# Both ends of a compressed-interaction kernel: the first weight row is loaded and summed earlier, and the last piece becomes 8 samples

## The chip, the cores and the metric

The kernel runs on one core of a Trainium2 chip. Its metric is the device time of one execution, in microseconds (us); four runs of the kernel before gave 485.12 to 485.51, median 485.37. One execution was profiled. The engines are named as the profile names them: PE (TensorE, the matrix products) and PEld (its weight loads), DVE (VectorE), ACT (ScalarE), POOL (GpSimd) and SP (SyncE, which here only issues transfers).

## The reference

A compressed interaction network of three layers over x, of shape (1024 samples, 64 fields, 16 embedding columns), all in float32:

```
x0 = h = x
for i in 0, 1, 2:                      # 128 output channels each
    z = einsum('bfe,bge->bfge', x0, h) # all pairs of fields
    y = einsum('oc,bce->boe', W_i, z.reshape(B, f0 * fh, E)) + b_i
    if i < 2: x_i, h = y[:, :64], y[:, 64:]
    else:     x_i = h = y
pooled = sum over e of concat(x_0, x_1, x_2)
out = pooled @ fc_w.T + fc_b           # (1024, 1)
```

The result is one number per sample. Since everything after layer 1 enters it only through fc_w, the kernel folds layer 2 and the pooled halves of the layers into small weight matrices, which it makes at its start.

## The kernel before

**Tiling.** The 1024 samples are 32 chunks of CB = 32 samples. A chunk has N = 512 columns (32 samples by 16 embedding columns). The pairs of fields of a chunk are 16 tiles of 128 rows by 512 columns: NJ = 4 groups j of NI = 4 tiles. The tiles of a group are one product on DVE or POOL (function product, L232): xa, the chunk's fields in four rotations, times one rotated copy xb of it, broadcast over the four. On PE, contract (L250 to L257) multiplies each of the 16 tiles of z by a 128x128 tile of w_all and adds them up in PSUM. The profile has two records, each with a weight load of its own (PEld), for one such float32 product.

**The start.** W0 comes in group by group as wh (the first tile row, 256 KB) and w0r (the other three, 768 KB). For each group, h1_weights (L352) adds the two mirrored halves of W0, one of which ACT first copies to PSUM (w0o). The first four chunks in HEAD order (2, 3, 0, 1) run a first half of the work (half_contract, L295) while the folded weights are made: PE makes the shifted copies xp of chunk 2 and 3 out of xa (L202), the products of W2 and W1 run between them (L408, L432), the result goes through DRAM (md) and comes back as ms, and DVE adds it into w_all (L531). After that head_q (L313) finishes chunks 0 and 1, and the other chunks go through contract.

**Order.** The order is written out by hand: each engine runs its instructions as the program lists them, and the loads are issued by SP in the order of load_xa, load_xb and the other dma_start calls. A transfer uses one of eight semaphores in turn, so a transfer can also wait for the landing of the one that used its semaphore last. The first transfers are xa of chunk c0 (first quarter, then the other three quarters), wh, the first quarter of xa of chunk c1, w0r, and so on.

**Around the change at the start** (L358 to L380): ACT copies a shifted tile for POOL (xb_gps), POOL multiplies group 1 of chunk c0 in two halves, DVE makes the products of group 0 for tile 0, then tile 1, then w_all's first row (after ACT's copy to w0o[0]), then the products for tiles 2 and 3. half_contract(c0, 0) on PE needs both.

**The end.** The last chunk, 31, is accumulated in two pieces (parts, in new_acc), 16 samples or 256 columns each (H2). For each chunk or piece, factors (L323) has ACT copy q out of PSUM (L329) and DVE multiply (L335); sums (L342) reduces over the 16 embedding columns (L344) into acc. pool (L605) sums over the channels by a product with ones on PE, into po; finish (L612) adds the constant cst on ACT and issues the output transfer. Before the change, the quarters of the output for all pairs of chunks but the last are pooled between the groups j = 1 and j = 2 of the second piece, and finished beside the rest of it. The last pair of chunks follows after the second piece: ACT copy, DVE product, DVE sum, pool on PE, bias on ACT, transfer on ACT's queue.

Of the kernel before, what the change touches and what calls it, by code (L numbers as in the profile page):

```python
# [37 lines left out]
F32 = mybir.dt.float32  # L38
AF = mybir.ActivationFunctionType
ALU = mybir.AluOpType  # L40
# [5 lines left out]
CB = 32  # L46
N = CB * E
H2 = N // 2
NCH = B // CB
NI = 4  # L50
NJ = 4
# [12 lines left out]
def cin_kernel(ctx, tc, xra, xrb, wh, w0r, w1h, w2t, wx1, wx0, vec, out):  # L64
# [109 lines left out]
    w2s = [flat_tile(f"w2_{k}") for k in range(2)]  # L174
    w1s = set_tile("w1s")
    load_xa(c0, slice(0, 1))
    load_xa(c0, slice(1, 4))
    nc.sync.dma_start(out=w0t[:, 0, :], in_=wh)
    load_xa(c1, slice(0, 1))
    nc.sync.dma_start(out=w0t[:, 1:NJ, :], in_=w0r)  # L180
    load_xa(c1, slice(1, 4))
# [35 lines left out]
    def new_acc(c, n=N, tag="acc"):  # L217
        if c == NCH - 1:
            parts[c] = [
                (ps.tile([128, H2], F32, tag=tag, name=f"acc_{c}_{n}", bufs=bufs), cols)  # L220
                for n, (tag, bufs, cols) in enumerate(
                    (("acc", 4, slice(0, H2)), ("set", 2, slice(H2, N)))
                )
            ]
            return
        accs[c] = ps.tile([128, n], F32, tag=tag, name=f"acc_{c}", bufs=4 if tag == "acc" else 2)

    def product(c, j, first=0, last=NI, engine=nc.vector):
        if first == 0:
            zs[c, j] = z_tile(f"z_{c}_{j}")  # L230
        at = slice(first, last)
        engine.tensor_tensor(  # L232
            zs[c, j][:, at, :], xas[c][:, at, :],
            xbs[c][j].unsqueeze(1).to_broadcast([128, last - first, N]), ALU.mult,
        )
        if j == NJ - 1:
            nc.scalar.activation(zs[c, j][SQ, 0, :], xas[c][SQ, 0, :], AF.Square)  # L237
# [12 lines left out]
    def contract(c, j, piece=0):  # L250
        acc_c, cols = pieces(c)[piece]
        for i in tiles(j):
            t = j * NI + i
            nc.tensor.matmul(  # L254
                acc_c, w_all[:, t, w_cols(c)], zs[c, j][:, i, cols],
                start=(t == 0 and c % 4 < 2), stop=(t == NT - NI and c % 4 >= 2),
            )  # L257
# [65 lines left out]
    def factors(c, which=slice(0, 1)):  # L323

        uu = uu_tile(c // 2)[halves[c % 2], 0, :]
        h = halves[c % 2]
        for acc_c, cols in pieces(c)[which]:
            q = sp.tile([128, N], F32, tag="q", name=f"q_{c}_{cols.start}")
            nc.scalar.copy(q[h, cols], acc_c[64 - h.start : 128 - h.start])  # L329
# [5 lines left out]
            nc.vector.scalar_tensor_tensor(  # L335
                uu[:, cols], acc_c[h], bh1[h], q[h, cols], ALU.add, ALU.mult
            )
# [4 lines left out]
    def sums(k, rows=slice(0, 128), of=slice(0, 2), half=slice(0, CB)):  # L342

        nc.vector.tensor_reduce(  # L344
            acc[rows, of, k, half],
            uus[k][rows, of, E * half.start : E * half.stop].rearrange("p k (b e) -> p k b e", e=E),
            AX.X,
            ALU.add,
        )

    def h1_weights(j, other=None):
        nc.vector.tensor_tensor(  # L352
            w_all[:, j * NI : (j + 1) * NI, 0:64], w0s[j][:, :, 0, :],
            w0s[j][:, :, 1, :] if other is None else other, ALU.add,
        )


    new_acc(c0, H2)  # L358
    nc.scalar.copy(xb_gps[:, 0, :], xbs[c0][1])  # L359
    xbs[c0][1] = xb_gps[:, 0, :]  # L360
    for i in (0, 2):
        product(c0, 1, i, i + 2, engine=nc.gpsimd)
    w0p = ps.tile([128, 2, NI, F], F32, tag="set", name="w0p")
    w0q = misc.rearrange("p (j i g) -> p j i g", i=NI, g=F)
    w0o = [w0p[:, 0], w0p[:, 1], w0q[:, 0], w0q[:, 1]]
    product(c0, 0, 0, 1)
    product(c0, 0, 1, 2)
    nc.scalar.copy(w0o[0], w0s[0][:, :, 1, :])
    h1_weights(0, w0o[0])
    product(c0, 0, 2, NI)  # L370
    nc.scalar.copy(w0o[1], w0s[1][:, :, 1, :])
    product(c0, 2, 0, 2)
# [232 lines left out]
    def pool(k0, k1, part=0, **flags):  # L605
        g, at = k0 // QP, slice(k0 % QP, (k1 - 1) % QP + 1)
        nc.tensor.matmul(  # L607
            po[32 * g : 32 * g + 2, at, :], ones, acc[:, part, k0:k1, :],
            tile_position=(0, 32 * g), skip_group_check=True, **flags,
        )  # L610

    def finish(k0, k1, queue):  # L612
        g, at = k0 // QP, slice(k0 % QP, (k1 - 1) % QP + 1)
        rows = slice(32 * g, 32 * g + 2)
        nc.scalar.activation(
            res[rows, at, :], po[rows, at, :], AF.Identity, bias=cst[rows]
        )
        queue.dma_start(out=outs[:, k0:k1, :], in_=res[rows, at, :])


# [1 line left out]
    for s, c in enumerate(order):  # L622
        k, head = c // 2, c in HEAD
        if order[s - 1] in HEAD and not head:
            for n in range(NF // 2):
                x_v0x(n)
            for n in HEAD:
                factors(n)
                if n % 2:
                    sums(n // 2)  # L630
        if 0 < s < len(order) - 2 and s not in (2, 3):
            load_products(*order[s + 2 : s + (4 if s == 6 else 3)])
        if s in (2, 3):

            if s == 2:
                for n in order[4:6]:
                    load_chunk(n)
                load_shared(0)
            for j in (0, 1) if s == 2 else (2, 3):
                for n in order[4:6]:  # L640
                    product(n, j)
        if s == len(HEAD) + 5:

            pc = ps.tile([128, 1], F32, tag="set", name="pc")
            for j in range(2):
                nc.tensor.matmul(
                    pc, fcol[:, j : j + 1].to_broadcast([128, 128]), bcol[:, j : j + 1],
                    start=(j == 0), stop=(j == 1),
                )
# [31 lines left out]
    po = ps.tile([128, QP, CB], F32, tag="set", name="po")  # L681
    quarters = [(k, min(k + QP, NP - 1)) for k in range(0, NP, QP)]
# [91 lines left out]
```

## Time and profile before

| what | value |
|---|---|
| median of four runs | 485.37 us |
| the profiled execution's own time | 485.12 us |
| its span in the profile | 483.3 us |
| PE busy | 477.2 us, 99% of the span |
| DVE, ACT, POOL busy | 368.8, 67.3, 15.3 us |
| bytes moved, mean rate | 87.01 MB, 180 GB/s |
| first product of half_contract on PE | 7.36 us |
| end of the last product column | 479.19 us |
| start of the last output transfer's issue | 481.27 us |

The profile is one execution. Its span begins with the first instruction and ends with the last; 1.8 us of the execution's time lie around it. A busy PE is not a PE at its peak, since products are pipelined. "The chain" is the work that ended last, followed back step by step to what released it: time that is on it counts, and time of an engine off it costs nothing unless something else then waits.

### The profile page before, as it was taken

Reading aid. Unit: us, or ns where it says so; the run is one execution under the profiler, and the core shown is the slowest. Engines: PE = TensorE matmul, PEld = TensorE weight load, DVE = VectorE, ACT = ScalarE, POOL = GpSimd, SP = SyncE. Lnnn points to the kernel's source line nnn. Section 1 sums busy time; section 2 is a strip of 40 time slices with the busy share of each in tenths; the row PEclk is TensorE's granted clock in tenths of the full one; section 3 lists DMA queues with packets and bytes.
Section 4 is the critical chain, followed back from the end, with each engine's and each line's share of the span. In section 5 each row is a group of like instructions: output and inputs, shape, how many; then the busy total and the mean of one; then the engine's idle time right before and its main releaser. Section 6 shows DMA issues by size and latency. Waiting matters only on the chain.

```text
span 483.3 us, 4409 instructions
## 1 busy us (share of the span) xinstructions
PE 477.2 (99%) x1802; PEld 217.3 (45%) x1802; DVE 368.8 (76%) x227; ACT 67.3 (14%) x142; POOL 15.3 (3%) x15
## 2 busy tenths in 40 slices
PE   8999999999999999999999999999999999999996
PEld 4564344443344444444444444444444444444465
DVE  5993799998899988898887686766868677771312
ACT  3242033011110111001100101001010011000002
POOL 5330000000000000000000000000000000000000
PEclk9999999999999999999999999999999999999999
DMA  8985997662952682587246344463246540000000
GB/s 335 403 277 175 391 378 279 219 215 108 353 236 87 228 285 111 196 268 283 107 171 210 142 174 175 171 213 105 120 174 224 210 147 28 0 1 0 0 1 1
DMA packets 19514, 87.01 MB, mean 180 GB/s; under 512 B 4802, under 2 KB 5474, under 8 KB 10598
## 3 DMA queue, kind: packets, MB, share of 16 engines
q1 hardware_dynamic: 18434, 85.71, 48.8%
q10 hardware_dynamic: 1060, 1.02, 0.8%
q8 instruction: 14, 0.23, 0.2%
q14 instruction: 6, 0.05, 0.0%
HBM read 85.08 MB, written 1.64 MB: 179 GB/s over the span
## 4 chain that ended last, share of the span: by engine, by line
PE 97%; DMA 1%; DVE 1%; ACT 0%; SPq 0%; issue 0%
PE acc L254 80%; PE acc L313 6%; PE acc L295 6%; PE acc L270 3%; PE acc L283 1%; DMA w0t<-in_wh 1%; PE xp L202 0%; PE pm L432 0%; PE pv L408 0%; PE y L275 0%; DVE z L232 0%; SPq L135 0%; PE po L607 0%; DVE uu L335 0%; DVE acc L344 0%
## 5 line engine op out<-in xcount | busy, mean ns | idle before, releaser
L254 PE MATMUL acc<-z,w_all 128*128 128x512 f32 (+1 forms) x928 | 387.5, 579 | 0.0
L232 DVE TENSOR_TENSOR z<-xa,xb 128x2048 f32<-128x2048 f32 x124 | 278.3, 2287 | 41.8 <-PE acc L254 35.1
L254 PEld LDWEIGHTS acc<-z,w_all 128*128 128x128 f32 x928 | 175.4, 190 | 210.8 <-issue 204.4
L237 ACT ACTIVATE z<-xa 32x512 f32<-32x512 f32 x34 | 21.3, 626 | 336.8 <-DVE z L232 334.8
L335 DVE SCALAR_TENSOR_TENSOR uu<-acc,vs,q 64x512 f32<-64x512 f32 (+1 forms) x29 | 21.2, 731 | 58.0 <-ACT q L329 57.8
L295 PE MATMUL acc<-z,w_all 128*64 128x256 f32 x256 | 29.0, 381 | 1.3 <-DVE w_all L352 1.3
L313 PE MATMUL acc<-z,w_all 128*64 128x512 f32 x128 | 27.9, 593 | 0.0
L232 DVE TENSOR_TENSOR z<-xa,xp 128x2048 f32<-128x2048 f32 (+2 forms) x12 | 20.4, 1749 | 5.3 <-PE xp L202 5.3
L295 PEld LDWEIGHTS acc<-z,w_all 128*64 128x64 f32 x256 | 17.9, 137 | 13.5 <-issue 2.5
L329 ACT COPY q<-acc 64x512 f32<-64x512 f32 (+1 forms) x33 | 18.7, 567 | 37.4 <-PE acc L254 21.4
L344 DVE TENSOR_REDUCE acc<-uu 128x64 f32<-128x1024 f32 (+3 forms) x19 | 20.3, 1073 | 0.3
L313 PEld LDWEIGHTS acc<-z,w_all 128*64 128x64 f32 x128 | 9.1, 137 | 18.0 <-issue 16.8
L275 PE MATMUL y<-xr,v0w 32*64 32x512 f32 x128 | 15.9, 600 | 0.0
L270 PE MATMUL acc<-xr,v1w 32*64 32x512 f32 (+1 forms) x132 | 15.7, 587 | 0.0
L340 DVE SCALAR_TENSOR_TENSOR uu<-y,cx,xx 128x512 f32<-128x512 f32 x16 | 11.3, 747 | 0.2
L270 PEld LDWEIGHTS acc<-xr,v1w 32*64 32x64 f32 x132 | 5.1, 131 | 9.9 <-issue 9.6
L232 POOL TENSOR_TENSOR z<-xa,xb_gps 128x1024 f32<-128x1024 f32 (+1 forms) x3 | 9.3, 3105 | 4.4 <-ACT xb_gps L359 3.8
L283 PE MATMUL acc<-sq,w_sq 32*64 32x512 f32 (+1 forms) x132 | 8.7, 574 | 0.0
L531 DVE TENSOR_TENSOR w_all<-ms 128x256 f32<-128x256 f32 x4 | 1.6, 424 | 5.2 <-DMA ms<-md 5.1
L166 ACT ACTIVATE sq<-xr 128x512 f32<-128x512 f32 x8 | 5.0, 630 | 3.5 <-DMA xr<-in_xra 3.3
L283 PEld LDWEIGHTS acc<-sq,w_sq 32*64 32x64 f32 x132 | 3.4, 132 | 3.8 <-issue 3.5
L232 POOL TENSOR_TENSOR z<-xa,xb 128x2048 f32<-128x2048 f32 x1 | 4.6, 4581 | 13.9 <-DMA xb<-in_xrb 13.9
(56 smaller groups left out, 66.8 us busy)
## 6 DMA issues: line engine op xcount, KB each, us to landing
xa<-in_xra SPq DMA_DIRECT2D x32, 1024.0 KB, 4.9
xb<-in_xrb SPq DMA_DIRECT2D x31, 1024.0 KB, 7.6
xr<-in_xra SPq DMA_DIRECT2D x32, 128.0 KB, 7.5
xx<-in_xra SPq DMA_DIRECT2D x32, 128.0 KB, 7.7
w<-in_w2t SPq DMA_DIRECT2D x2, 1024.0 KB, 10.9
xa<-in_xra SPq DMA_DIRECT2D x2, 768.0 KB, 7.9
w1s<-in_w1h SPq DMA_DIRECT2D x1, 1024.0 KB
w1x<-in_wx SPq DMA_DIRECT2D x1, 1024.0 KB
```

Of the source, the lines that this page charges most:

```text
L232: engine.tensor_tensor(zs[c, j][:, at, :], xas[c][:, at, :], xbs[c][j].unsqueeze(1).to_broadcast([128, last - first, N]), ALU.mult,)
L237: nc.scalar.activation(zs[c, j][SQ, 0, :], xas[c][SQ, 0, :], AF.Square)
L254: nc.tensor.matmul(acc_c, w_all[:, t, w_cols(c)], zs[c, j][:, i, cols], start=(t == 0 and c % 4 < 2), stop=(t == NT - NI and c % 4 >= 2),)
L270: nc.tensor.matmul(acc_c[halves[1 - n]], v1w[at, m], xr[:, cols], start=(m == 0 and c not in ends), stop=False, tile_position=(at.start, 6 ...
L275: nc.tensor.matmul(ys[c // 2][halves[n]], v0w[at, m], xr, start=(m == 0), stop=(m == 1), tile_position=(at.start, 64 * n),)
L283: nc.tensor.matmul(acc_c[halves[n]], w_sq[at, w_cols(c)][:, 64 * n : 64 * n + 64], sqs[first][at, cols], start=h and (first == 0 or c not ...
L295: nc.tensor.matmul(accs[c][halves[n]], w_all[:, t, 0:64], zs[c, j][:, i, n * H2 : (n + 1) * H2], start=(t == 0), stop=(j == last and i == ...
L313: nc.tensor.matmul(accs[c][halves[1 - c % 2]], w_all[:, t, 64:128], zs[c, j][:, i, :], start=(t == 0), stop=False,)
L329: nc.scalar.copy(q[h, cols], acc_c[64 - h.start : 128 - h.start])
L335: nc.vector.scalar_tensor_tensor(uu[:, cols], acc_c[h], bh1[h], q[h, cols], ALU.add, ALU.mult)
L340: nc.vector.scalar_tensor_tensor(uu_tile(k)[:, 1, :], ys[k], cx, xxs[k], ALU.add, ALU.mult)
L344: nc.vector.tensor_reduce(acc[rows, of, k, half], uus[k][rows, of, E * half.start : E * half.stop].rearrange("p k (b e) -> p k b e", e=E), ...
```

## The change

At the start, wh is loaded as the second transfer, directly after the first quarter of chunk c0's xa, and the rest of that xa follows as two transfers (one quarter, then two). ACT's copy to w0o[0] and DVE's sum of w_all's first row stand before xb_gps and before the first product. POOL's group is three products (two tiles, one, one) instead of two.

At the end, the two pieces of chunk 31 have 24 and 8 samples (384 and 128 columns) instead of 16 and 16. The sums of chunk 30, the pooling of all earlier pairs of chunks, and their bias and output transfers stand within the first piece. The bias of the last pair is added on DVE instead of ACT, and its output transfer is issued by SP instead of ACT.

```
+CUT = 24
...
     load_xa(c0, slice(0, 1))
-    load_xa(c0, slice(1, 4))
     nc.sync.dma_start(out=w0t[:, 0, :], in_=wh)
+    load_xa(c0, slice(1, 2))
+    load_xa(c0, slice(2, 4))
     load_xa(c1, slice(0, 1))
     nc.sync.dma_start(out=w0t[:, 1:NJ, :], in_=w0r)
...
-                (ps.tile([128, H2], F32, tag=tag, name=f"acc_{c}_{n}", bufs=bufs), cols)
+                (ps.tile([128, cols.stop - cols.start], F32, tag=tag, name=f"acc_{c}_{n}", bufs=bufs), cols)
                 for n, (tag, bufs, cols) in enumerate(
-                    (("acc", 4, slice(0, H2)), ("set", 2, slice(H2, N)))
+                    (("acc", 4, slice(0, E * CUT)), ("set", 2, slice(E * CUT, N)))
...
     new_acc(c0, H2)
-    nc.scalar.copy(xb_gps[:, 0, :], xbs[c0][1])
-    xbs[c0][1] = xb_gps[:, 0, :]
-    for i in (0, 2):
-        product(c0, 1, i, i + 2, engine=nc.gpsimd)
     w0p = ps.tile([128, 2, NI, F], F32, tag="set", name="w0p")
...
+    nc.scalar.copy(w0o[0], w0s[0][:, :, 1, :])
+    h1_weights(0, w0o[0])
+    nc.scalar.copy(xb_gps[:, 0, :], xbs[c0][1])
+    xbs[c0][1] = xb_gps[:, 0, :]
+    for i in ((0, 2), (2, 3), (3, 4)):
+        product(c0, 1, *i, engine=nc.gpsimd)
     product(c0, 0, 0, 1)
     product(c0, 0, 1, 2)
-    nc.scalar.copy(w0o[0], w0s[0][:, :, 1, :])
-    h1_weights(0, w0o[0])
     product(c0, 0, 2, NI)
...
-    def finish(k0, k1, queue):
+    def finish(k0, k1, queue, engine=nc.scalar):
...
+        if engine is nc.scalar:
+            engine.activation(res[rows, at, :], po[rows, at, :], AF.Identity, bias=cst[rows])
+        else:
+            engine.tensor_scalar(res[rows, at, :], po[rows, at, :], cst[rows], None, ALU.add)
...
+            if c == NCH - 1:
+                factors(c - 1)
+                sums(k, of=slice(1, 2))
+                sums(k, slice(0, 64), slice(0, 1))
+                done = acc[:, :, 0:k, :]
+                nc.vector.tensor_tensor(done[:, 0], done[:, 0], done[:, 1], ALU.add)
+                po = ps.tile([128, QP, CB], F32, tag="set", name="po")
             for j in range(NJ):
                 contract(c, j)
+                if c == NCH - 1 and j == 1:
+                    quarters = [(n, min(n + QP, k)) for n in range(0, NP, QP)]
+                    for at in quarters:
+                        pool(*at, start=True, stop=True)
+                    pool(k, NP, 1, start=True, stop=False)
+                    for at in quarters:
+                        finish(*at, nc.sync)
...
-        if c == HEAD[0] or c % 4 in (0, 3) and s and order[s - 1] not in HEAD:
+        if c == HEAD[0] or c % 4 in (0, 3) and s and order[s - 1] not in HEAD and c < NCH - 1:
...
-    sums(NP - 1, of=slice(1, 2))
-    sums(NP - 1, slice(0, 64), slice(0, 1))
+    first, last = slice(0, CUT), slice(CUT, CB)
     factors(NCH - 1)
-    sums(NP - 1, slice(64, 128), slice(0, 1), slice(0, CB // 2))
-    done = acc[:, :, 0 : NP - 1, :]
-    nc.vector.tensor_tensor(done[:, 0], done[:, 0], done[:, 1], ALU.add)
+    sums(NP - 1, slice(64, 128), slice(0, 1), first)
     for j in range(NJ):
-        if j == 2:
-            for at in quarters:
-                pool(*at, start=True, stop=True)
-            pool(NP - 1, NP, 1, start=True, stop=False)
         contract(NCH - 1, j, 1)
-    for at in quarters:
-        finish(*at, nc.sync)
     factors(NCH - 1, slice(1, 2))
-    sums(NP - 1, slice(64, 128), slice(0, 1), slice(CB // 2, CB))
+    sums(NP - 1, slice(64, 128), slice(0, 1), last)
     pool(NP - 1, NP, start=False, stop=True)
-    finish(NP - 1, NP, nc.scalar)
+    finish(NP - 1, NP, nc.sync, nc.vector)
```

More of the change, by code (lines that the diff above doesn't have):

```diff
@@ L610, in pool @@
         )
-    def finish(k0, k1, queue):
+    def finish(k0, k1, queue, engine=nc.scalar):
         g, at = k0 // QP, slice(k0 % QP, (k1 - 1) % QP + 1)
         rows = slice(32 * g, 32 * g + 2)
-        nc.scalar.activation(
-            res[rows, at, :], po[rows, at, :], AF.Identity, bias=cst[rows]
-        )
+        if engine is nc.scalar:
+            engine.activation(res[rows, at, :], po[rows, at, :], AF.Identity, bias=cst[rows])
+        else:
+            engine.tensor_scalar(res[rows, at, :], po[rows, at, :], cst[rows], None, ALU.add)
         queue.dma_start(out=outs[:, k0:k1, :], in_=res[rows, at, :])
@@ L679, in cin_kernel @@
             sums(k - 1)
-    po = ps.tile([128, QP, CB], F32, tag="set", name="po")
-    quarters = [(k, min(k + QP, NP - 1)) for k in range(0, NP, QP)]
-    sums(NP - 1, of=slice(1, 2))
-    sums(NP - 1, slice(0, 64), slice(0, 1))
+    first, last = slice(0, CUT), slice(CUT, CB)
     factors(NCH - 1)
-    sums(NP - 1, slice(64, 128), slice(0, 1), slice(0, CB // 2))
-    done = acc[:, :, 0 : NP - 1, :]
-    nc.vector.tensor_tensor(done[:, 0], done[:, 0], done[:, 1], ALU.add)
+    sums(NP - 1, slice(64, 128), slice(0, 1), first)
     for j in range(NJ):
-        if j == 2:
-            for at in quarters:
-                pool(*at, start=True, stop=True)
-            pool(NP - 1, NP, 1, start=True, stop=False)
         contract(NCH - 1, j, 1)
-    for at in quarters:
-        finish(*at, nc.sync)
     factors(NCH - 1, slice(1, 2))
-    sums(NP - 1, slice(64, 128), slice(0, 1), slice(CB // 2, CB))
+    sums(NP - 1, slice(64, 128), slice(0, 1), last)
     pool(NP - 1, NP, start=False, stop=True)
-    finish(NP - 1, NP, nc.scalar)
+    finish(NP - 1, NP, nc.sync, nc.vector)
 def kernel(r_x, L0_rec_W0, L0_rec_b0, L0_rec_W1, L0_rec_b1, L0_rec_W2, L0_rec_b2, L0_rec_fc_w, L0_rec_fc_b):
```

## The prediction

> **What bounds the kernel now.** I read the page first: the busy line and the chain that ended last.
>
> ```profile
> PE 477.2 (99%) x1802; PEld 217.3 (45%) x1802; DVE 368.8 (76%) x227; ACT 67.3 (14%) x142; POOL 15.3 (3%) x15
> ...
> PE 97%; DMA 1%; DVE 1%; ACT 0%; SPq 0%; issue 0%
> ```
>
> TensorE is the chain for 97% of the span, and the edits leave its number of instructions and columns as they were. So only the two ends can move. I took the same chain in order of time, first its start (start us, us, what):
>
> ```profile
> 1.68 4.77 DMA w0t<-in_wh
> 6.46 0.02 issue
> 6.48 0.39 ACT w0p L368
> 6.86 0.02 issue
> 6.89 0.42 DVE w_all L352
> 7.31 1.14 DVE z L232
> 8.45 0.04 issue
> 8.49 1.08 PE acc L295 x8
> ```
>
> The reader sees the first tile row of W0 landing at 6.45, its sum ready at 7.31, and a product that ends only at 8.45 because VectorE made the sum in front of it. From 8.49 on, every piece of the chain is TensorE until 479.19. Its end:
>
> ```profile
> 475.53 3.67 PE acc L254 x16
> 479.19 0.02 issue
> 479.22 0.37 ACT q L329
> 479.59 0.03 issue
> 479.61 0.50 DVE uu L335
> 480.12 0.02 issue
> 480.14 0.43 DVE acc L344
> 480.56 0.14 issue
> 480.70 0.23 PE po L607 x2
> 480.93 0.02 issue
> 480.96 0.28 ACT res L615
> ```
>
> After the last product column, five instructions run one after another on 256 columns (16 samples), then the output goes out. Last, the timeline, for the waits that a quicker start would meet:
>
> ```profile
> 9.25 0.38 ACT L371 COPY w0p<-w0t 128x256 f32<-128x256 f32 x1 [2.40 <-DMA w0t<-in_w0r]
> ...
> 9.66 0.42 DVE L352 TENSOR_TENSOR w_all<-w0t,w0p 128x256 f32<-128x256 f32 x1
> ...
> 44.06 1.21 DVE L531 TENSOR_TENSOR w_all<-ms 128x256 f32<-128x256 f32 x3 [4.18 <-DMA ms<-md]
> ```
>
> **The change part by part.** The sum is made against the profiled execution: 485.12 us, of which the span is 483.3 and 1.8 lie around it. It is the lowest of the four runs (median 485.37), so a gain found in it is taken off the median.
>
> *Start, arrival.* The 256 KB of W0 now follow the first 256 KB of xa instead of the first 1024 KB. The windows show 367 to 431 GB/s between 3 and 8 us; the 786 KB (decimal) no longer in front are 1.9 us at 410. So it lands at 6.45 - 1.9 = 4.6 instead of 6.45. The xa rest moves behind it, to about where W0 landed: 6.5.
>
> *Start, order.* ACT's copy (0.38) runs at 4.6 to 5.0: ACT is done with the vs copy at 4.33, and the xb_gps copy now behind it can't start before 5.32 anyway (it waits for the shifted tile from PE), so POOL's start at 6.04 stays. VectorE adds at 5.03 to 5.45. Behind this add, with its new wait, the first product is queued: 5.26 becomes 5.4. From start to start VectorE needs 0.34 for the add and 0.61 for a 128x512 product (records of the timeline), so the 128x1024 product starts at about 6.6, when its xa has landed, and ends 1.21 later at 7.8 instead of 8.44. PE's chain would start 0.65 sooner.
>
> *Start, what is late next.* PE then does 1.02 of products and 1.02 of shifts and wants the second tile row of w_all at 9.9. That row is in the third fence: ACT waits for w0r until 9.25, VectorE adds until 10.08. The bytes before w0r are the same, so this doesn't move, but for the split of xa: eight packets of 2 KB and eight of 4 KB for eight of 6 KB on each engine; 6 KB took 236 ns and 2 KB 84, which makes about 0.07 us. PE goes on at 10.15 to 10.2 instead of 10.53. I take -0.33. Bounds: -0.41 (no cost of the split) and -0.1 (w0r 0.3 late, one 256 KB transfer of this trace having taken 0.2 more than another).
>
> *Is it kept?* What PE meets next, less 0.33: chunk c0's last product ended at 14.32 and was wanted at 15.20; chunk 1's first at 34.10, wanted at 34.83; the sum at 44.06 at 44.49, wanted at 45.17 (slack 0.68, the least). All hold. After 60 us products are 2 to 38 us ahead. POOL's third product, now in two halves, ends at 10.74 plus a fixed cost of some 0.1, wanted at 11.4. The added transfer shifts the semaphores by one, so the w2 load now waits for vs (landed 4.09) before it is issued; the queue has work for another 6 us, as the windows show its engines fully busy from 3 to 20 us.
>
> *Last chunk, PE.* 64 records of 256 columns become 32 of 384 and 32 of 128. 128 records of 512 columns took 55.13 us in the chain, 0.431 each, so 0.215 for 256, 0.323 for 384 and, by columns, 0.108 for 128. But every record brings a 128x128 weight load that lasts 190 ns by its row. Whether these overlap is shown at one place, three loads in front of one-column products:
>
> ```profile
> 174.57 0.41 PEld L646 LDWEIGHTS pc<-vs 128*128 128x128 f32 x3 [0.24 <-issue]
> ```
>
> Three loads of 0.19 in 0.41: one every 0.11. So a 128-column record takes 0.112, not 0.108: +0.13 over the piece. Bounds: 0 (columns alone) and 0.190 a record (no overlap), +2.6. The zero products at L107 have the very form, 128x128 by 128 columns, at 3.22 us for 14, 0.23 each; but their loads took 333 ns where the same load later takes 190, so PE was slower there, and I take the row that is later and quicker.
>
> A rule speaks against this piece. The Trainium skill (TensorE: Matmul & The Clock Gate, Back-to-back issue gap) says that in a stream of weight loads and products a 128-column product costs about 81 ns where its columns alone would take 56. With two passes a record that would be 0.162 a record, +1.7 us, and the kernel slower; its figure for 512 columns, 131 ns a pass, is not what this trace has (0.431 a record), so I stay with the row.
>
> *Last chunk, what moves.* The pooling products move from the second piece into the first, at the same cost; they need VectorE's chain for chunk 30 (465.49 + 0.74 + 1.26 + 0.66 = 468.1), and PE gets there at 464.7 + 16 x 0.323 = 469.9. ACT's four bias operations (1.49) and SP's four output transfers (1.67) follow at 470, hidden by products until 475.5. ACT's copy, VectorE's product and sum of the first piece (about 0.47, 0.62 and 0.54) must fit beside 3.6 us of the second piece, and do.
>
> *Tail.* For 128 columns by the line through the two forms measured: ACT's copy 0.580 at 512 and 0.364 at 256, so 0.256 (-0.11); VectorE's product 0.749 and 0.490, so 0.36 (-0.13); its sum 0.667 and 0.416, so 0.29 (-0.125). The bias on VectorE has no row: its 32x64 memset in PSUM took 0.112, its 64x32 copy 0.188, and the line of the product meets zero columns at 0.23. I take 0.23, the only one with a per-partition scalar from PSUM, against ACT's 0.281 (-0.05; bounds -0.17 and +0.05). The last transfer goes out by SP: by the landings recorded, SP's four took 1.10 to 1.17 from issue, ACT's 1.10: zero, 0.1 either way. Sum of the tail: -0.41.
>
> *Sum.* -0.33 + 0.13 - 0.41 = -0.61: the median 485.37 becomes 484.75.
>
> **The rivals.**
> 1. *Weight loads set the last piece* (slower). For: each takes 190 ns, of the 215 that a 256-column record lasts. Against: L646. Price at 0.190 a record: 32 x 0.078 = +2.5, so 487.25. Above 0.131 a record the gains are used up, above 0.161 the kernel is slower by more than 0.2%.
> 2. *The start is taken back*: w0r lands later, or the sum of the ms rows (44.06) or chunk 1's first product comes 0.35 to 0.4 late, and PE waits there instead. For: these are the least slacks, and all hang on DMA. Against: m_sb is written sooner too. Only the tail is left, +0.13 - 0.41: 485.1.
> 3. *Both ends at their best*: no cost of the split, columns alone in the piece, the bias as short as the memset: -0.41 - 0.53 = -0.94, and with 0.1 from the SP queue 484.3.
>
> **How the numbers follow.** 0.2% is 0.97 us, about what a measurement of this kernel can tell from no change. Forecast 62%, rival 2 15%, rival 3 13%, rival 1 10%. The forecast's own spread (its bounds make about 0.3 either way) puts a tenth of it under 484.4. So faster 20%, same 70%, slower 10%. The range runs from 484.2 (rival 3) to 485.7 (rival 2 with a wait of 0.6 more) and leaves out rival 1.
>
> **What would show it.** Right: the first w_all sum before 5.5; PE's first products at about 6.1 and the second row's at 10.2; no TensorE gap near 42 to 45; weight loads of the last piece 0.11 apart; chain steps after it of about 0.26, 0.36, 0.29 and 0.23. Wrong: loads 0.16 or more apart, a VectorE wait that PE meets before 45 us, or an SP issue that lands later than ACT's did.

## The result, and the profile after

The median went from 485.45 us (53 runs beside it) to 485.98 us (33 runs): a ratio of 1.0013, 95% interval 1.0008 to 1.0018. A gain of 0.61 us was forecast; a loss of 0.53 us came, and 485.98 lies above the upper end of the range (485.7). The loss is smaller than the 0.2% that the prediction took as what a measurement can tell from no change, but the whole interval lies above 1. The profiled execution of the changed kernel took 485.85 us, with a span of 484.1. Six of the 34 executions on record took 487.3 to 487.6 us at a mean granted clock of 0.996, the others 485.5 to 486.3 at 0.998 or more; the experiments come back to them.

First the page of the changed kernel, its busy line and the shares of the chain:

```profile
PE 477.9 (99%) x1802; PEld 215.2 (44%) x1802; DVE 369.2 (76%) x228; ACT 66.9 (14%) x141; POOL 15.4 (3%) x16
...
PE 97%; DMA 1%; DVE 0%; SPq 0%; issue 0%; ACT 0%
```

TensorE is the bound as before, so again only the two ends count. The chain of work that ended last, of the changed kernel, start and end (start us, us, what):

```profile
2.15 5.89 DMA xa<-in_xra
8.04 0.02 issue
8.06 1.23 DVE z L234
9.29 0.04 issue
9.34 1.08 PE acc L297 x8
10.42 1.02 PE xp L204 x8
11.44 0.13 issue
11.57 1.95 PE acc L297 x16
...
43.04 13.73 PE acc L315 x64
...
471.47 8.94 PE acc L256 x48
480.41 0.02 issue
480.43 0.27 ACT q L331
...
480.72 0.37 DVE uu L337
...
481.12 0.29 DVE acc L346
...
481.54 0.23 PE po L609 x2
...
481.80 0.26 DVE res L620
```

The same mark in the chain of the kernel before, where the group of L315 is that of L313:

```profile
41.91 13.73 PE acc L313 x64
```

The chain no longer begins with W0 but with the rest of xa (its second to fourth quarter), which lands at 8.04 instead of 5.79. PE's first group over it starts at 9.34 instead of 8.49, 0.85 later, and the group of L315 at 43.04 instead of 41.91, so 1.13 lost. The end is shorter: from 480.41 to the span's end at 484.1 are 3.7 us, where it was 4.1 (479.19 to 483.3). PE itself needs 437.37 us from 43.04 to 480.41, and needed 437.28. So +1.13 + 0.09 - 0.4 = +0.8: the two spans differ by 0.8, the times of the two profiled executions by 0.73.

The timeline of the changed kernel shows who waits for what (start us, us, engine, line; in brackets the idle time before and what ended it):

```profile
4.61 0.38 ACT L364 COPY w0p<-w0t 128x256 f32<-128x256 f32 x1 [0.26 <-DMA w0t<-in_wh]
...
8.06 2.35 DVE L234 TENSOR_TENSOR z<-xa,xp 128x1024 f32<-128x1024 f32 x2 [1.18 <-DMA xa<-in_xra]
...
9.34 1.08 PE L297 MATMUL acc<-z,w_all 128*64 128x256 f32 x8 [1.75 <-DVE z L234]
...
10.59 0.38 ACT L373 COPY w0p<-w0t 128x256 f32<-128x256 f32 x1 [4.35 <-DMA w0t<-in_w0r]
```

W0's first row is there at 4.6, as meant. But VectorE then waits 1.18 for the rest of xa, PE 1.75 for VectorE, and the second row of W0 is copied at 10.59 instead of 9.25: 1.34 later, though the bytes in front of it are the same. VectorE's sum of this row ends at 11.42 (11.00 + 0.42), just as PE, delayed by the rest of xa, gets there at 11.44; PE goes on at 11.57. So most of the loss on the chain is the rest of xa; the second row is ready just when the delayed PE reaches it.

Where that came from shows in the windows view (a stretch in us; its length and the busy us of PE, PEld, DVE, ACT, POOL; granted clock; DMA share; GB/s). Before the change:

```profile
4.00:5.00 1.00, 0.94 (x8) 0.47 (x12) 0.00 (x0) 0.22 (x1) 0.00 (x0) 1.00 1.00 412
5.00:6.00 1.00, 1.00 (x12) 0.16 (x4) 0.74 (x2) 0.59 (x1) 0.00 (x0) 1.00 0.97 367
6.00:8.00 2.00, 0.72 (x10) 0.49 (x8) 1.66 (x3) 0.38 (x1) 1.96 (x1) 1.00 1.05 423
```

After it:

```profile
4.00:5.00 1.00, 0.93 (x8) 0.38 (x12) 0.00 (x0) 0.59 (x2) 0.00 (x0) 1.00 1.03 328
5.00:6.00 1.00, 1.00 (x16) 0.27 (x8) 0.82 (x2) 0.34 (x1) 0.00 (x0) 1.00 0.84 277
6.00:8.00 2.00, 1.59 (x12) 0.40 (x8) 0.88 (x2) 0.24 (x1) 1.62 (x1) 1.00 1.00 368
```

The last column is the point: 328 and 277 GB/s instead of 412 and 367. The DMA share stays near 1 (0.84 at the least), so most DMA engines are occupied, but some of their packets last longer. In the trace's packet records a packet of 2 and 6 KB takes 84 and 234 ns at the median of either kernel between 3 and 8 us, one of 4 KB 159 in the changed one. In this stretch 2 packets before the change took over 330 ns (the longest 385), and 19 after it (the longest 712). A transfer has landed when the last of its 16 completions has come, and these spread out: for w0r from 9.03 to 10.51 after the change, from 8.51 to 9.17 before it. The first one is 0.52 later, the last one 1.34.

### The profile page after: what moved, and what is told of

Read it like the earlier page. It is cut to its first block, busy times and chain, and to the rows that moved or that the text cites. A ratio compares the mean times of both kernels' runs of the same rounds, so it can differ in the third digit from the quotient of the medians.

```text
span 484.1 us, 4412 instructions
## 1 busy us (share of the span) xinstructions
PE 477.9 (99%) x1802; PEld 215.2 (44%) x1802; DVE 369.2 (76%) x228; ACT 66.9 (14%) x141; POOL 15.4 (3%) x16
## 4 chain that ended last, share of the span: by engine, by line
PE 97%; DMA 1%; DVE 0%; SPq 0%; issue 0%; ACT 0%
PE acc L256 80%; PE acc L297 6%; PE acc L315 6%; PE acc L272 3%; PE acc L285 1%; DMA xa<-in_xra 1%; PE xp L204 0%; PE pv L410 0%; PE pm L434 0%; DVE z L234 0%; PE y L277 0%; SPq L136 0%; PE po L609 0%; SPq L178 0%; DVE uu L337 0%
## 5 line engine op out<-in xcount | busy, mean ns | idle before, releaser
L256 PE MATMUL acc<-z,w_all 128*128 128x512 f32 (+2 forms) x928 | 387.6, 579 | 0.0
L256 PEld LDWEIGHTS acc<-z,w_all 128*128 128x128 f32 x928 | 173.1, 190 | 213.0 <-issue 204.9
L337 DVE SCALAR_TENSOR_TENSOR uu<-acc,vs,q 64x512 f32<-64x512 f32 (+2 forms) x29 | 21.2, 731 | 57.8 <-ACT q L331 57.6
L315 PE MATMUL acc<-z,w_all 128*64 128x512 f32 x128 | 27.9, 593 | 0.0
L331 ACT COPY q<-acc 64x512 f32<-64x512 f32 (+2 forms) x33 | 18.7, 566 | 35.9 <-PE acc L256 19.8
L346 DVE TENSOR_REDUCE acc<-uu 128x64 f32<-128x1024 f32 (+4 forms) x19 | 20.3, 1073 | 0.3
L315 PEld LDWEIGHTS acc<-z,w_all 128*64 128x64 f32 x128 | 9.1, 137 | 18.0 <-issue 17.9
L272 PE MATMUL acc<-xr,v1w 32*64 32x512 f32 (+2 forms) x132 | 15.7, 587 | 0.0
L234 POOL TENSOR_TENSOR z<-xa,xb_gps 128x512 f32<-128x512 f32 (+2 forms) x4 | 9.4, 2362 | 5.5 <-ACT xb_gps L366 4.1
L285 PE MATMUL acc<-sq,w_sq 32*64 32x512 f32 (+2 forms) x132 | 8.7, 574 | 0.0
```

The costliest lines, as they stand in the source:

```text
L234: engine.tensor_tensor(zs[c, j][:, at, :], xas[c][:, at, :], xbs[c][j].unsqueeze(1).to_broadcast([128, last - first, N]), ALU.mult,)
L256: nc.tensor.matmul(acc_c, w_all[:, t, w_cols(c)], zs[c, j][:, i, cols], start=(t == 0 and c % 4 < 2), stop=(t == NT - NI and c % 4 >= 2),)
L272: nc.tensor.matmul(acc_c[halves[1 - n]], v1w[at, m], xr[:, cols], start=(m == 0 and c not in ends), stop=False, tile_position=(at.start, 6 ...
L285: nc.tensor.matmul(acc_c[halves[n]], w_sq[at, w_cols(c)][:, 64 * n : 64 * n + 64], sqs[first][at, cols], start=h and (first == 0 or c not ...
L315: nc.tensor.matmul(accs[c][halves[1 - c % 2]], w_all[:, t, 64:128], zs[c, j][:, i, :], start=(t == 0), stop=False,)
L337: nc.vector.scalar_tensor_tensor(uu[:, cols], acc_c[h], bh1[h], q[h, cols], ALU.add, ALU.mult)
```

## Experiments

Each kernel was measured beside 15 to 53 executions of the kernel before. The ratio compares all executions with those, so that where the times of one kernel lie far apart (in the last two rows most of all) it is not the quotient of the medians. The table gives, for the profiled execution, the rate between 4 and 8 us and when the last of a transfer's 16 completions came (us); the time is the median over all executions. "Rest" is the second to fourth quarter of the xa of chunk 2 (c0), or its last part, "row 2" is w0r, which brings W0's second row.

| kernel | GB/s, 4 to 8 | rest | row 2 | median us | ratio to before (95%) |
|---|---|---|---|---|---|
| before | 406 | 5.79 | 9.17 | 485.45 | |
| after | 335 | 8.04 | 10.51 | 485.98 | 1.0013 (1.0008 to 1.0018) |
| end_only | 406 | 5.96 | 9.17 | 485.08 | 0.999 (0.998 to 1.0) |
| start_only | 323 | 8.15 | 10.60 | 486.18 | 1.0015 (1.0002 to 1.0027) |
| one_rest | 311 | 8.78 | 11.25 | 486.82 | 1.0035 (1.0018 to 1.0052) |
| before_split | 347 | 6.79 | 9.87 | 486.21 | 1.0017 (1.0004 to 1.0031) |
| wh_act | 415 | 6.35 | 8.94 | 485.81 | 1.0008 (0.9999 to 1.0017) |
| after_own | 414 | 7.31 | 9.82 | 486.28 | 1.0015 (1.0006 to 1.0024) |
| one_rest_own | 425 | 7.20 | 9.69 | 486.20 | 1.0015 (1.0006 to 1.0024) |
| end_own | 416 | 6.80 | 9.94 | 486.18 | 1.0015 (1.0006 to 1.0023) |
| rest_own | 414 | 7.00 | 9.49 | 487.89 | 1.0047 (1.0033 to 1.006) |
| rest_own_split | 387 | 6.95 | 9.60 | 485.83 | 1.0006 (0.9998 to 1.0015) |
| rest_own_end | 411 | 5.85 | 8.99 | 484.88 | 0.9994 (0.9983 to 1.0004) |
| split_own | 312 | 7.27 | 10.35 | 486.14 | 1.0023 (1.0014 to 1.0032) |
| gate_rest | 308 | 8.03 | 10.49 | 485.87 | 1.0011 (1.0002 to 1.002) |
| gate_xa | 310 | 6.92 | 11.35 | 486.70 | 1.0028 (1.0018 to 1.0037) |
| after_fill | 327 | 8.07 | 10.53 | 485.69 | 1.0008 (1.0 to 1.0017) |
| rest_own_split_fill | 304 | 8.17 | 10.65 | 485.88 | 1.0011 (1.0002 to 1.002) |
| wh_first | 394 | 8.66 | 11.13 | 485.00 | 0.9994 (0.9985 to 1.0003) |
| wh_first_fill | 393 | 6.80 | 9.25 | 486.31 | 1.0009 (0.9997 to 1.0021) |

One execution of one_rest_own took 1310.73 us, which nothing on record explains; it counts in the median, not in the ratio. The rates and landings are of one execution each.

### Each end alone

`end_only` is the changed kernel with the transfers and the order of the start as before (shown are the transfers; the copies, the sum and the products of the start are put back too):

```
     load_xa(c0, slice(0, 1))
-    nc.sync.dma_start(out=w0t[:, 0, :], in_=wh)
-    load_xa(c0, slice(1, 2))
-    load_xa(c0, slice(2, 4))
+    load_xa(c0, slice(1, 4))
+    nc.sync.dma_start(out=w0t[:, 0, :], in_=wh)
```

> Start as before the change, end as after it. Theory A (the start costs what the end gains and more): the tail after the last product column is 3.65 us instead of 4.12 and the second piece costs PE about 0.1, so 0.3 to 0.45 us less than before, a ratio of 0.9991 to 0.9994; the second tile row of W0 is summed at about 9.7 us as before. Rival (the last piece itself costs): no gain or a loss, 1.000 or more, with the loss to be seen between the last chunk's first product and the last product column.

`start_only` is the opposite: the start as changed, the end as before.

> Start as after the change, end as before it. Theory A: the second tile row of W0 lands at about 10.5 us instead of 9.2, PE's first product of a full chunk (at 55.6 us before) starts about 1.1 later, and the time is 0.9 to 1.2 us over before: 1.0019 to 1.0025. Rival (chance in the profiled execution): the row lands at 9.2 to 9.5 and the time is 0 to 0.4 us under before.

Measured: 0.37 us under and 0.73 us over the kernel before. The chain of end_only:

```profile
470.57 8.94 PE acc L255 x48
479.52 0.02 issue
479.54 0.27 ACT q L330
...
480.91 0.26 DVE res L619
```

The last 48 products (16 of 384 columns, 32 of 128) take the same 8.94 as in the changed kernel, and the span ends at 483.2, 3.7 us after the last of them. The interval of end_only just reaches 1.0, but nine of its 11 executions took 485.10 or less, and four of the 53 of the kernel before. In start_only the rest lands at 8.15 and the second row at 10.60, as in the changed kernel. So the end is the gain that it was forecast to be, and the start alone costs. It was not chance in one profile: four kernels with this order of the first transfers and the same sources (after, start_only, after_fill, gate_rest) have the rest at 8.03 to 8.15 and the second row at 10.49 to 10.60.

### Which part of the new order costs

`one_rest` keeps W0's first row in the second place, but the rest of xa is one transfer:

```
     nc.sync.dma_start(out=w0t[:, 0, :], in_=wh)
-    load_xa(c0, slice(1, 2))
-    load_xa(c0, slice(2, 4))
+    load_xa(c0, slice(1, 4))
```

> As after the change, but the rest of the first xa is one transfer of 768 KB (6 KB pieces) behind the 256 KB of W0, not two of 256 and 512 KB. Theory A (several small transfers issued one behind the other keep the queues poorly filled): the xa rest lands at 6.5 to 6.8 us, the second tile row of W0 at 9.2 to 9.5, and the time is 0.5 to 0.7 us under before, 0.9985 to 0.999. Rival B (it is the order, W0 in the second place, that costs): landings stay at 8.0 and 10.5 and the time stays as after the change, 1.0010 to 1.0018.

`before_split` keeps the order of before (and the new end), but cuts the rest in two:

```
     load_xa(c0, slice(0, 1))
-    load_xa(c0, slice(1, 4))
+    load_xa(c0, slice(1, 2))
+    load_xa(c0, slice(2, 4))
     nc.sync.dma_start(out=w0t[:, 0, :], in_=wh)
```

> Start as before, but with the rest of the first xa split into 256 and 512 KB (W0's 256 KB behind it as before); end as after the change. Theory A (number of small transfers): the second tile row of W0 lands 0.7 to 1.3 us later than 9.17 and the time is 0.4 to 1 us over that of the kernel with only the end changed. Rival B (order): within 0.1 us of that kernel.

`wh_act` has one rest directly behind the first quarter on SP's queue, and sends W0's first row by ACT's queue, behind vs:

```
     nc.scalar.dma_start(out=vs, in_=vec)
+    w0t = z_tile("w0t")
+    nc.scalar.dma_start(out=w0t[:, 0, :], in_=wh)
```

> As the kernel with one rest, but W0's 256 KB go out on ACT's queue behind vs, so that on SP's queue the rest of xa follows its first quarter directly, as before the change. Theory D (what stands between the two xa transfers on their queue): the rest lands by 6.8, the second tile row by 9.4, 0.5 to 0.8 us under before. Theory C (shared rows out of step): stalls stay, landings at 7.5 to 8.8 and 10 to 11, at or above before.

Either part is enough. With W0 between, one rest lands at 8.78, and the kernel is the slowest of the three; with the cut alone, the kernel is 1.1 us over end_only. In wh_act, which has neither on SP's queue, the rate stays at 415 GB/s and the rest lands at 6.35. Its time is not better all the same: on two queues W0's first row lands only at 6.55, and the sum that now stands in front of the products holds these up (products of L314, which is L313 before, from 43.19). So "many small transfers" (theory A) is wrong as a reason of its own, since one_rest has as many as the kernel before, and "W0 in the second place" (B) is not the only one. Nor is it the new order of the engines' work at the start: before_split has the old one.

### Do packets that read the same rows stall one another?

xra has 132 rows of 2 KB per chunk, and partition p reads rows p to p+3, so the transfers of xa read rows again that others read. In `after_own`, `one_rest_own` and `end_own`, all of chunk 2's xa comes from an array in which each partition has its own 8 KB; in `rest_own`, `rest_own_split`, `rest_own_end` and `split_own` only the rest does, with 6 KB a partition, in the orders of one_rest, after, end_only and before_split.

```
+        "xar": xra[HEAD[0], np.arange(128)[:, None] + np.arange(1, NI)],
...
+    def load_rest(at):
+        nc.sync.dma_start(out=xas[c0][:, at, :], in_=xar[:, at.start - 1 : at.stop - 1, :])
```

> As after the change, but chunk 2's xa is read from an array of its own, in which every partition has its 8 KB, so that no two packets read the same row of DRAM (xra has 132 rows, and partition p reads rows p to p+3, so that neighbours and the three transfers share rows). Theory C (packets that read the same rows stall one another when the transfers are no longer in step): no packet over 0.35 us between 4 and 7 us, over 380 GB/s there, the xa rest landed by 6.9 and the second tile row of W0 by 9.4, and 0.5 to 0.8 us under before, 0.9983 to 0.999. Theory A/D (the number or the order of the transfers): landings at 8.0 and 10.5, time as after the change, 1.0008 to 1.0018.

> As the kernel with one rest of 768 KB behind W0's 256 KB, but with chunk 2's xa from an array of its own, without shared rows. Theory C: no long packets, xa rest by 6.8 and the second tile row by 9.4, the clock full from 4 us on, 0.6 to 0.8 us under before, 0.9983 to 0.9988. Theory D (order): as the kernel with one rest, 486.2 to 487, with landings at 8.8 and 11.

> As the kernel with only the end changed, but with chunk 2's xa from an array of its own. Control of the array itself: under every theory the landings stay as in that kernel to 0.15 us (xa rest 5.8 to 6.0, second tile row 9.1 to 9.3), and the ratio is 0.9988 to 0.9995.

> As the kernel with one rest behind W0's 256 KB, but only the rest of chunk 2's xa (6 KB of each partition) comes from an array of its own; the first quarter comes from xra as before. Theory C (shared rows stall packets that are out of step; a first transfer from the spread array starts slower, 127 to 165 GB/s in 2 to 3 us): first quarter at 3.9 to 4.1, W0's first row at 4.6, the rest at 6.4 to 6.8, the second row at 9.1 to 9.4, PE's first product over a full z row 0.5 to 0.7 earlier than before, time 0.5 to 0.8 us under before: 0.9983 to 0.999. Rival (any new array brings a slow start): first quarter after 4.5, second row 9.6 or later, 1.0005 to 1.0015.

> As after the change, to the letter but that the two transfers of the rest (256 and 512 KB) come from an array without shared rows. Theory C: no long packets after 4 us, rest by 6.9, second row of W0 by 9.5, time 0.3 to 0.7 under before (0.9985 to 0.9995), so 0.9 to 1.3 under after. Theory A (the number of transfers): rest at 7.5 to 8, 1.0005 or more.

> As the kernel with only the end changed, with the rest of chunk 2's xa from an array of its own. Control: landings as in that kernel (first quarter 3.9, rest 5.8, W0's first row 6.5 to 6.7, second row 9.2), ratio 0.9988 to 0.9995. If the new array itself costs, the rest lands after 6.2 and the ratio is over 1.

> As the kernel with the order of before, the rest of the first xa split into 256 and 512 KB and the end of after the change (486.2, 1.1 over the same kernel without the split), but with these two transfers read from an array without shared rows. Theory C (shared rows stall one another): the loss goes, 484.9 to 485.3, second row of W0 at 9.1 to 9.5. Theory A (the number of small transfers): the loss stays, 485.9 to 486.4.

The first three looked like a proof: between 4 and 8 us no packet took over 330 ns, at 414 to 425 GB/s. But all three have this, the control end_own too, and they have something else in common: their first transfer is slow (246 to 249 GB/s between 3 and 4 us, where the changed kernel has 368), and the first quarter lands at 4.7 to 4.95 instead of 3.9. Their medians are 0.7 to 0.8 over before, where a gain was expected. The chain of after_own shows what the late quarter does:

```profile
0.74 4.02 DMA xa<-in_xah
4.76 0.14 issue
4.90 3.50 PE xp L209 x16
```

PE makes the shifted tiles in 3.50 us, where it took 2.02 before the change: in these three the granted clock becomes full only at 8.08 to 9.32 us, and at 3.63 to 6.47 in the other profiles. So they test the shared rows and a late start at once, and settle nothing on the rows. Of the next three, rest_own_end, the control, lands as expected (rest 5.85, second row 8.99), so the new array costs nothing in this place; rest_own_split looked right in its one profile (484.90) and not in its median (485.83). `split_own` decides. Its chain:

```profile
2.16 5.75 DMA w0t<-in_wh
7.91 0.02 issue
7.93 0.39 ACT w0p L373
...
8.76 1.14 DVE z L237
```

W0's first row, which follows the rest there, lands at 7.91 instead of 6.45, without a shared row in the rest, and the time is that of before_split (486.14 and 486.21). Theory C falls: the loss comes without shared rows. rest_own is also a warning: its profiled execution was the fastest of five (485.28), three of the others took 487.9 to 488.3.

### The loads issued meanwhile

In the changed kernel, SP's issues of the loads of W2 and W1 took 0.43 to 1.05 us each, against 0.42 to 0.44 before, in the time of the long packets. `gate_rest` keeps them away from it by a transfer of 128 bytes out of the last part of xa, for which SP has to wait:

```
+    gate = dr.tile([1, 32], F32, tag="gate", name="gate")
+    nc.sync.dma_start(out=gate, in_=xas[c0][0:1, 2, 0:32])
     for k in range(2):
         nc.sync.dma_start(out=w2s[k], in_=w2t[k])
```

> As after the change, with a transfer of 128 bytes out of the last-loaded part of chunk 2's xa on SP's queue ahead of the loads of W2 and W1, so that SP issues these (1 MB each) only when the rest of xa has landed, instead of from 4.1 us on. Theory F (the transfers being served are held up while SP issues further ones: SP's issues of W2 and W1 took 0.5 to 1.3 us there against 0.42 before the change): no packets over 0.35 us from 4 to 7 us, the rest at 6.4 to 7.0, the second row of W0 at 9.1 to 9.6, time 0.3 to 0.8 under before. Rival (it is the order of the transfers themselves): rest at 8.0 to 8.2, second row at 10.4 to 10.7, time as after the change or up to 0.3 over it.

`gate_xa` puts it further ahead, before `load_xa(c1, slice(0, 1))`, and lets it wait for the first quarter.

> As after the change, with the same small transfer further ahead: it waits for the first quarter of xa (3.9 us), and the first quarter of chunk 3's xa and everything behind it is issued after that, from 4.4 us on instead of 2.6. Theory F: if only the issues of the loads behind count, the stalls move or stay, since SP then issues from 4 to 7 us without a break: rest at 7 to 8.2. If it is the number of transfers open at once: no stalls, the rest at 6.4 to 7.0, the second row at 9.2 to 9.7. Rival (order): rest at 8.0 to 8.2.

In gate_rest SP issues nothing from 4.2 to 8.1 us, and the rest still lands at 8.03, the second row at 10.49, with 28 packets over 330 ns. Theory F falls for these loads: their long issues go with the long packets and are not the cause. In gate_xa the rest does land at 6.92, but the long packets are now in the transfers behind it (up to 1.24 us, when w0r's turn comes at 8 us), and the second row lands at 11.35, the latest of all. The stalls moved with the issuing; what they hang on is not settled by this.

### The clock, and the executions at 487

When the rest is late, PE waits. In one_rest's profiled execution (487.98) the granted clock changed at 6.13, 9.54 and 12.96 us; the windows view between these (columns as above, the clock ahead of the DMA share):

```profile
6.13:9.54 3.41, 1.40 (x12) 0.20 (x4) 1.24 (x3) 0.47 (x1) 0.59 (x1) 1.00 0.96 354
9.54:12.96 3.42, 3.40 (x16) 1.37 (x20) 3.42 (x4) 1.06 (x3) 3.42 (x3) 0.50 1.02 428
```

PE was busy for 1.40 of 3.41 us, and the next 3.41 us ran at half clock. In split_own a stretch with 1.71 of 3.41 (6.47 to 9.88) was followed by full clock. The first stretch at full clock begins at another time in every execution (3.63 to 6.47 us in 17 of the 20 profiles, later in the three with the late first quarter), so a gap of some 1.7 us, as the changed kernel has it, now and then falls so that it makes most of one stretch. For the changed kernel that is argued: its six executions at 0.996 were not traced. `after_fill` puts products of zeros, which add nothing, into this gap:

```
+                if (c, t) == (c0, 1):
+                    for _ in range(6):
+                        nc.tensor.matmul(
+                            accs[c][halves[0], 0:128], zeros[:, 0:64], zeros,
+                            start=False, stop=False,
+                        )
```

> As after the change, with six products of zeros on PE (about 1.3 us) put between the first two and the last two tiles of PE's first group, where PE waits for the rest of xa. Theory E (PE's idle time there lets the granted clock fall to one half for 3.41 us in executions whose 3.41 us windows lie badly, which costs 1.5 to 2 us): no execution at a mean clock of 0.996 and none over 486.6, the others as after the change, median 485.7 to 486.0. Rival (the slower executions come from the transfers): about one in six still at 487.3 or more. The transfers, unchanged, land late again: rest at 7.5 to 8.5, second row of W0 at 10 to 10.7.

`rest_own_split_fill` does so with three such products in rest_own_split.

> As after the change with the two transfers of the rest from an array without shared rows, with three products of zeros (about 0.7 us) in the same place of PE. If both causes are found (shared rows and PE's idle time): 484.9 to 485.6, none over 486.6, rest by 7 and second row of W0 by 9.7. If something else delays the transfers in most executions: 485.8 or more.

The timeline of after_fill:

```profile
7.27 1.49 PE L304 MATMUL acc<-const-float32-0.0 128*64 128x128 f32 x12
9.37 1.08 PE L297 MATMUL acc<-z,w_all 128*64 128x256 f32 x8 [0.60 <-DVE z L234]
```

PE's wait shrinks from 1.75 to 0.60. None of 11 executions has a mean clock of 0.996, none took over 486.16, and the median is 0.29 under the changed kernel, with the rest as late as ever (8.07). The second kernel has none over 486.17 either. This fits theory E, and so do the clocks on record: the 25 executions of all kernels with a mean clock of 0.996 or less, one of the kernel before among them, took 487.28 us or more. It is not proof: with six in 34, eleven in a row without one come by chance about one time in eight, and three executions of other kernels took 487.1 to 487.3 at 0.999 or 1.0. Nor is the half clock the main loss of the changed kernel: 485.69 is still 0.33 over the runs beside it (485.36). In the profile of rest_own_split_fill the long packets are back (304 GB/s, rest at 8.17), once more without shared rows in the rest.

### A better order?

`wh_first`, made from one_rest, puts W0's first row ahead of all, so that first quarter and rest of xa stay neighbours:

```
+    nc.sync.dma_start(out=w0t[:, 0, :], in_=wh)
     load_xa(c0, slice(0, 1))
-    nc.sync.dma_start(out=w0t[:, 0, :], in_=wh)
     load_xa(c0, slice(1, 4))
```

> As the kernel with one rest of 768 KB, but W0's 256 KB come first of all, ahead of the first quarter of xa, so that this quarter and the rest stand next to each other as before the change. Theory G (the stalls come when something stands between the first quarter and the rest, or when the rest is cut): no stalls, W0's first row at 3.9, the first quarter at 4.6, the rest at 6.3 to 6.8, the second row at 9.0 to 9.5; the shifted tiles come 0.6 later, and the time is 0.6 under to 0.2 over before. Rival (any order but that of before stalls): the rest at 7.5 or later, the second row at 10 or later, time 0.5 to 1.5 over before.

`wh_first_fill` adds two products of zeros behind each of the first two tiles.

> As the kernel with W0's 256 KB first of all, with two products of zeros (about 0.45 us) on PE behind each of the first two tiles of its first group. Its transfers in an ordinary execution, if theory G holds: W0's first row at 3.9, first quarter of xa 4.6, rest 6.3 to 6.8, second row 8.9 to 9.4, no packet over 0.6 us. Theory E (PE idle for over half of a 3.41 us window halves the clock for the next): no execution at a mean clock of 0.996 or less and none over 486.6, the median 484.6 to 485.2. Rival (a late transfer alone makes the slow executions): some still at 487 or more.

Six of 12 executions of wh_first took 484.64 to 484.72, 0.8 under the runs beside it (485.48): somewhat more than the prediction had promised for the change. The other six took 485.3 to 488.4; the slowest was the profiled one, in which one of the 16 completions of the rest came 2 us after the others (15 by 6.60, the last at 8.66) and the clock halved after it. wh_first_fill, which was to take the half clock away, shows the good case in its chain (484.94):

```profile
1.68 5.12 DMA xa<-in_xra
6.79 0.02 issue
6.82 0.70 DVE z L233
...
42.10 5.14 PE acc L320 x23
```

But only five of its 12 executions were under 485, seven lay at 486.3 to 487.3, without a half clock; what held these up no trace shows. So theory G holds for half of the executions at best: by the times, this order makes the stalls rarer, and doesn't exclude them. Of all versions, end_only and rest_own_end are under the median of before in most executions (nine and ten of 11); end_only has no execution over 485.55 and is the one to keep.

## Why the prediction was wrong

**The bound.** Right: TensorE is the chain for 97% after too, and only the ends moved.

**Start, arrival.** Right for W0: 4.59 (forecast 4.6); the first sum began at 5.02 and PE's products at 6.35 (forecast 6.1). Wrong for the rest of xa, which got no bound: "to about where W0 landed: 6.5" was 8.04.

**Start, order.** Right that the add holds up the first product little: it ended at 5.44, and the product then waited 0.16 more for the shifted tile (5.60, forecast 5.4), since the full clock came at 4.95 instead of 4.28 in this execution. The 128x1024 product started at 8.06 instead of 6.6, for the rest of xa alone, and PE's group behind it at 9.34 instead of about 7.8.

**Start, what is late next: the landings, here and under arrival, are the step that failed.** "The bytes before w0r are the same, so this doesn't move, but for the split of xa", priced at 0.07 us and bounded at 0.3. It moved by 1.34, and PE's products of the second row from 10.53 to 11.57. The term -0.33 was +1.13 in the profile, and +0.73 in start_only's median. Both landings, that of the rest (8.04 for 6.5) and that of w0r, were priced by the bytes in front of them at the rate of the old order. The rest is the one on the chain: 0.85 of the 1.13 is there when PE starts on it. The second row alone would have cost about as much, by argument: its sum ended at 11.42, and the forecast had PE want it at 9.9. The bytes were right; the rate was not: 335 instead of 406 GB/s between 4 and 8 us. The usual packets took what the sum assumed (84 and 234 ns at the median in either kernel); it had no term for a few long packets, after which the last of 16 completions comes late. Its bound was the scatter within the old order. The runs show that this order is a good case: a cut of the rest (before_split, split_own) or W0's row between (one_rest) is enough to lose it. Why, they don't show. Shared rows in the rest, the loads of W2 and W1 issued meanwhile, and the mere number of transfers are not needed for the loss.

**Is it kept?** Right as far as it goes: no gap of PE near 42 to 45 in the changed kernel. A loss at the start is kept: 1.13 at 43.04, and from this mark to its last column PE takes 437.37 us in the changed kernel and in end_only alike.

**Last chunk.** Right. The weight loads of the last piece came every 0.112, forecast 0.112; the piece cost 0.09 us, forecast 0.13 (bounds 0 and 2.6). The rule quoted from the Trainium skill (TensorE: Matmul & The Clock Gate, Back-to-back issue gap) would have made it 0.162 a record and +1.7 us by the prediction's estimate; these float32 records agree with it neither at 128 columns (0.112) nor at 512 (0.431).

**Tail.** Right. ACT's copy 0.26, VectorE's product 0.36, sum 0.28 and bias 0.26 (forecast 0.256, 0.36, 0.29, 0.23), SP's transfer 1.08 from issue to landing (1.10 on ACT's queue before). From the last column to the end of the span 4.1 became 3.7: -0.4, forecast -0.41.

**The rivals.** Rival 2 named the mechanism, w0r landing later, and priced it at the gain alone: it ended at "only the tail is left", 485.1. The range's upper end put 0.6 more on it, without a row for it; 1.13 was more. The prediction's own sign of being wrong, "a VectorE wait that PE meets before 45 us", came true: PE waited 1.75 us for VectorE at 9.34. Rivals 1 and 3 did not happen. That PE's wait could halve the clock was no rival at all: by the forecast's own numbers PE would have waited only from 7.2 to 7.8.

## What to carry to other kernels

A sum of bytes in front of a transfer prices its landing only as long as the rate holds, and at this kernel's start the rate hung on the order and the cut of the transfers. Price a reordering of the first loads with a loss of rate as one bound (here 15 to 25% over 4 us, which made a transfer behind them land 0.7 to 2.2 us later), not with the scatter of the old order. Test the two ends of such a change apart: here one was worth 0.4 us and was hidden by the other. And where several executions of one kernel form two groups, look at more than one profile before believing an explanation; rest_own_split and rest_own each had a single profile that pleased and a median that did not.

## What the runs showed of the hardware

- The transfers at the start can lose rate when their order or cut changes at equal bytes: 304 to 347 GB/s between 4 and 8 us in the profiles of nine kernels against 406 in the order of before, by single packets of 2, 4 or 6 KB that take up to 1.45 us instead of 84, 159 and 234 ns. In start_only six packets, begun between 5.05 and 5.22, all ended between 6.42 and 6.57. What releases them is open.
- An array of 8 KB a partition, of which the first transfer takes 2 KB each, delivers this first transfer 0.8 to 1.0 us later (4.7 to 4.95) than 128 neighbouring rows of 2 KB (3.9 before and after the change).
- The granted clock changes in steps of 3.41 us. It fell to one half after a stretch with PE busy for 1.40 us of it (one_rest), and after one with 0.76 (wh_first); it stayed after 1.71 (split_own, before_split). At the start it became full after a stretch with 2.85 us busy (wh_first), and not yet after one with 2.34 to 2.75 (end_own, one_rest_own, after_own). The Trainium skill (TensorE: Matmul & The Clock Gate, What's actually happening) tells of a free-running window of about 3.4 us, which agrees, and of a fall after an idle window; here a wait of 2.02 us within one window was enough (one_rest).
